# Left combinations of the split products formed in layer 0, products split from the second unit on, and w1 loaded a unit later

## The chip, the cores and the metric

The kernel runs on one core of one Trainium2 chip. The metric is the device time of one execution in microseconds (us). Times of a kernel are medians over several executions. One further execution was recorded by the hardware profiler; every row of a profile below is from that one execution.

## The reference

Two layers, each followed by a residual addition and a layer normalisation. All matrices are float32; N = 4096 nodes, D = 512 features. Cut to what matters:

```python
# layer 0
bw = sign(w0); ba = maximum(sign(x), 0)
x = layernorm(x + relu(adj @ (ba @ bw.T)))
# layer 1
node_att = softmax(x @ node_w, axis=0)
h = x @ edge_w
e = where(adj > 0, h @ h.T, -9e15)
support = x @ w1
out = (adj * node_att * softmax(e, axis=1)) @ support + bias
x = layernorm(x + out)
```

## The kernel before

The work is in four stages, one after the other on the tensor engine (PE).

**Layer 0** (0 to about 509 us). `xw = ba @ bw.T` is kept in SBUF. The 32 row blocks (128 rows each) of `adj @ xw` follow in the loop at L367. A row block has four quarters. In each, ScalarE (ACT) rounds a quarter of the adjacency tile `at` to `hi` (L385), VectorE (DVE) forms the rest `lo = at - hi` (L387), and PE multiplies both into the bank `acc` (L395, L396). `hi` and `lo` have two buffers each. What follows a row block (relu, residual, normalisation, node score, store of x1, transposes) is the generator `rest`. `step()` advances every unfinished `rest` once a quarter, after `lo` was formed, so the `rest` of block n runs in the four quarters of block n+1 and the first of n+2. Row blocks come in pairs; after the odd one of a pair, `left` (L338) forms the seven left operands of a Strassen-Winograd product (four additions of 128x256, L343 to L346) in the tile `sums_l`, and four DMAs of GpSimd's queue (L347 to L350) store them in `lop_d`. The order on DVE and ACT in this loop is the order in which the code is written (`manual_schedule`). DMAs that load `at` and `xb` are on SyncE's queue (SP), those that load pieces of the mask on ACT's queue, and all stores on GpSimd's queue (POOL).

**h** (509 to 606 us). `h = x1 @ edge_w` by the function `seven`, which calls `between_h` after each multiplication; DVE adds the seven products out of six PSUM banks.

**Scores** (606 to 1075 us). `h @ h.T`, masked row maxima and sums of exponentials, with the scores stored in `s_d`.

**Aggregation** (1075 us to the end). The product of the attention with x1, in 16 units `Aggregate(g, r)`: g is one of four groups of 1024 output rows, r one of four groups of 1024 terms of the sum, r innermost. A unit has seven products m (Strassen-Winograd on 2x2 blocks). The right operands are the weighted attention tiles `r11, r12, r21, r22` and the combinations t3, r12-r11, t2, t4 that `combine` forms on DVE (L896, L898, L901, L904; 128x2048 each). All of that for the next unit is done during a unit, by `steps()`: eight loads of 1 MB on POOL's queue (L858, L865), `shift` (DVE, L871), `exp` (ACT, L874), `clip` (ACT, L877), `weigh` (DVE, L883) and `combine`. For the first unit it is done at the end of the scores. The left operands are loaded from `lop_d` on SP's queue (L1097).

An unsplit product is 2 halves of 4 matmuls, 128x128 by 128x512 (L1117). A float32 matmul shows as two records in the trace, so this is 16 records. A **split** product is itself done by seven products of half the size: 14 matmuls by 128x256, 28 records. `SPLIT` names the three products m = 6, 4, 3 that are split, in the units for which `in_two(n)` holds, n = 4 to 14. A split product needs

- the right combinations of half size, `second` (DVE, L994 to L998, four of 128x512), in one of two tiles `extra` that are taken at unit 4;
- the left combinations of half size. `Aggregate.lefts` forms them once per r, in units 0 to 3 (g = 0), right after the product m whose left operand is in SBUF: four DVE instructions of 128x256 (L1007 to L1010), and two stores on ACT's queue (L1014) to `lop2_d`;
- from unit 4 on four loads per split product, L1101 to L1104, into two of the four `lop` buffers (`low`, `high`);
- four partial sums instead of two per product, each read back into a PSUM bank (`seed`, ACT, L1089) and written out again (`evict`, ACT, L1126); after the last unit of a g `join_inner` adds them up (21 additions of 128x256, L1165).

The program order in the aggregation is only a preference; the compiler's scheduler orders each engine's queue, except for instructions passed through `keep_in_program_order` (in unit 0: `pinned`). [...]

The matrix w1 is loaded into the tile `over` when the aggregation starts (L1391). `over` takes the place of `hT`, so the load waits for the last matmul of the scores. Four combinations of w1 (L1420 to L1423) are in the list `todo` of unit 1. They are used by `Finish` (L1244), the multiplication with w1 that follows each g.

## Time and profile before

| what | us |
|---|---|
| median of 3 runs | 1933.15 (1933.03 to 1934.24) |
| the profiled execution's own time | 1934.05 |
| span of its trace | 1932.3 |
| PE busy | 1913.5 |
| DVE busy | 1387.0 |
| ACT busy | 1024.3 |
| POOL busy | 280.5 |

The unit boundaries on PE, from the starts of the L1117 records (112 records in an unsplit unit, 148 in a unit with three split products):

| unit | PE from to, us | length |
|---|---|---|
| 0 | 1074.87 to 1126.85 | 51.98 |
| 1 | 1126.85 to 1174.92 | 48.07 |
| 2 | 1174.92 to 1222.98 | 48.06 |
| 3 | 1222.98 to 1271.92 | 48.94 |
| 4 | 1271.92 to 1323.57 | 51.65 |
| 5 | 1323.57 to 1383.50 | 59.93 |
| 7 | 1436.04 to 1482.51 | 46.47 |
| 11 | 1645.74 to 1692.21 | 46.47 |

Units 3, 7 and 11 hold 8 records of `panel` (L819) besides their own; units 4, 5 and others hold matmuls of `Finish`. In a timeline row the columns are start, length, engine, line and operation; in square brackets stands the idle time before it and what ended it. In a table of windows the columns are named in its first line; (x) is a count of instructions.

### The profile page before, as it was taken

Reading aid. Unit: us, or ns where it says so; the run is one execution under the profiler, and the core shown is the slowest. Engines: PE = TensorE matmul, PEld = TensorE weight load, DVE = VectorE, ACT = ScalarE, POOL = GpSimd, SP = SyncE. Lnnn points to the kernel's source line nnn. Section 1 sums busy time; section 2 is a strip of 40 time slices with the busy share of each in tenths; the row PEclk is TensorE's granted clock in tenths of the full one; section 3 lists DMA queues with packets and bytes.
Section 4 is the critical chain, followed back from the end, with each engine's and each line's share of the span. In section 5 each row is a group of like instructions: output and inputs, shape, how many; then the busy total and the mean of one; then the engine's idle time right before and its main releaser. Section 6 shows DMA issues by size and latency. Waiting matters only on the chain.

```text
span 1932.3 us, 20169 instructions
## 1 busy us (share of the span) xinstructions
PE 1913.5 (99%) x6708; PEld 1200.9 (62%) x6708; DVE 1387.0 (72%) x2058; ACT 1024.3 (53%) x1619; POOL 280.5 (15%) x409
## 2 busy tenths in 40 slices
PE   8999999999999999999999999999999999999998
PEld 6888888888644455444555444456666666666655
DVE  6766676666765567566664986687869987798746
ACT  5433333333202567576777665546767577757731
POOL 0122122222321101011111111111101101111100
PEclk9999999999999999999999999999999999999999
DMA  8888888888585478577773998787778787887731
GB/s 311 285 328 308 306 311 307 328 308 292 176 280 198 157 259 312 188 276 253 294 301 113 347 327 285 271 283 246 259 266 292 259 279 260 301 283 258 274 109 44
DMA packets 169527, 508.72 MB, mean 263 GB/s; under 512 B 15696, under 2 KB 41040, under 8 KB 161744
## 3 DMA queue, kind: packets, MB, share of 16 engines
q1 hardware_dynamic: 89472, 226.39, 34.6%
q0 software_dynamic: 64688, 239.10, 33.1%
q10 hardware_dynamic: 15264, 41.95, 6.0%
q8 instruction: 53, 0.87, 0.2%
q14 instruction: 50, 0.41, 0.1%
HBM read 385.74 MB, written 121.63 MB: 263 GB/s over the span
## 4 chain that ended last, share of the span: by engine, by line
PE 90%; DVE 4%; DMA 2%; issue 2%; ACT 1%; POOL 0%; ACTq 0%; DVEq 0%; POOLq 0%
PE bank L1117 33%; PE seven L749 14%; PE acc L395 11%; PE acc L396 11%; PE pe L676 6%; PE seven L101 5%; PE po L1244 3%; PE pt L638 3%; DMA slot<-s_d 1%; PE pt L355 1%; PE acc L236 1%; PE acc L235 1%; PE pw L213 1%; DMA over<-in_w_dram 1%; PE bank L1244 0%
## 5 line engine op out<-in xcount | busy, mean ns | idle before, releaser
L1117 PE MATMUL bank<-lent,lop 128*128 128x512 f32 (+1 forms) x1136 | 420.0, 517 | 0.0
L395 PE MATMUL acc<-xw,hi 128*128 128x512 f32 x960 | 376.5, 392 | 0.0
L396 PE MATMUL acc<-xw,lo 128*128 128x512 f32 x960 | 373.9, 390 | 0.0
L1117 PE MATMUL bank<-slot,lop 128*128 128x256 f32 (+1 forms) x1052 | 357.8, 488 | 1.9 <-DVE slot L898 1.9
L1117 PEld LDWEIGHTS bank<-lent,lop 128*128 128x128 f32 x1136 | 215.7, 190 | 173.9 <-issue 159.5
L1117 PEld LDWEIGHTS bank<-slot,lop 128*128 128x128 f32 x1052 | 200.2, 191 | 136.7 <-issue 116.6
L385 ACT CAST hi<-at 128x1024 fp32r<-128x1024 f32 x120 | 126.4, 1053 | 203.6 <-PE acc L395 152.9
L387 DVE TENSOR_TENSOR lo<-at,hi 128x1024 fp32r<-128x1024 f32 x120 | 148.0, 1233 | 85.7 <-ACT hi L385 85.7
L396 PEld LDWEIGHTS acc<-xw,lo 128*128 128x128 f32 x960 | 180.3, 188 | 36.8 <-DVE lo L387 0.3
L395 PEld LDWEIGHTS acc<-xw,hi 128*128 128x128 f32 x960 | 180.3, 188 | 36.8
L1126 ACT COPY over<-bank 128x512 f32<-128x512 f32 x200 | 115.0, 581 | 117.3 <-PE bank L1117 103.8
L676 PE MATMUL pe<-hT 128*128 128x512 f32 (+3 forms) x384 | 132.1, 486 | 0.0
L609 ACT ACTIVATE line<-line,nmax_c 128x512 f32<-128x512 f32 x160 | 114.8, 725 | 22.5 <-DVE nmax_c L600 22.3
L600 DVE CUSTOM_DVE_ANT_0 line<-lent,slot 128x512 f32<-128x512 bf16 x140 | 90.7, 688 | 47.7 <-ACT slot L686 26.7
L877 ACT ACTIVATE slot<-slot 128x2048 f32<-128x2048 f32 x36 | 68.8, 1911 | 73.6 <-DMA slot<-in_adj_t_dram 73.6
L871 DVE CUSTOM_DVE_ANT_1 lent<-lent,line 128x2048 f32<-128x2048 f32 x40 | 91.2, 2283 | 17.0 <-ACT line L831 8.6
L874 ACT ACTIVATE lent<-lent 128x2048 f32<-128x2048 f32 x40 | 76.5, 1913 | 49.1 <-DVE lent L871 49.0
L676 PEld LDWEIGHTS pe<-hT 128*128 128x128 f32 x384 | 64.6, 191 | 41.4 <-issue 33.8
L749 PE MATMUL seven<-hT 128*128 128x512 f32 x192 | 89.8, 593 | 0.0
L1089 ACT COPY bank<-over 128x512 f32<-128x512 f32 x144 | 84.7, 597 | 2.9 <-DVE left L1009 0.2
L638 PEld LDWEIGHTS pt<-ident,lent 128*128 128x128 f32 x418 | 52.3, 141 | 52.2 <-issue 38.3
L639 ACT COPY slot<-pt 128x512 f32<-128x512 f32 (+3 forms) x123 | 68.5, 560 | 22.9 <-PE pt L638 22.9
(261 smaller groups left out, 2828.2 us busy)
## 6 DMA issues: line engine op xcount, KB each, us to landing
at<-in_adj_t_dram SPq DMA_DIRECT2D x60, 1024.0 KB, 7.3
lop<-lop_d SPq DMA_DIRECT2D x79, 512.0 KB, 4.7
lent<-s_d POOLq DMA_DIRECT2D x39, 1024.0 KB, 7.3
slot<-in_adj_t_dram POOLq DMA_DIRECT2D x38, 1024.0 KB, 6.8
s_d<-slot POOLq DMA_DIRECT2D x30, 1024.0 KB, 7.2
lent<-in_adj_t_dram POOLq DMA_DIRECT2D x26, 1024.0 KB, 7.1
lop<-lop_d SPq DMA_DIRECT2D x99, 256.0 KB, 4.1
lent<-in_adj_dram SPq DMA_DIRECT2D x48, 512.0 KB, 5.0
```

The costliest lines, as they stand in the source:

```text
L101: nc.tensor.matmul(banks[bank][q], lop(m, q)[k], rop(m)[k], start=(first and k == 0), stop=(k == K - 1), skip_group_check=not first,)
L385: nc.scalar.copy(hi, aq)
L387: nc.vector.tensor_sub(lo, aq, hi.bitcast(F32))
L395: nc.tensor.matmul(acc, hi[:, c, :], xw[:, kb, :], start=(kb == 0), stop=False)
L396: nc.tensor.matmul(acc, lo[:, c, :], xw[:, kb, :], start=False, stop=(kb == NB - 1))
L609: nc.scalar.activation(line, line, AF.Exp, bias=nmax_c[:, b, c : c + 1], scale=-1.0, accum_out=sum_c[:, b, c : c + 1])
L638: nc.tensor.transpose(pt[:, j, :], src[:, ts(j, P)], ident)
L676: nc.tensor.matmul(pe[:, lo * P :], hT[:, k, ts(A * BG + i, P)], hT[:, k, (B * BG + lo) * P : (B + 1) * W], start=(k == 0), stop=(k == KD ...
L749: nc.tensor.matmul(ps, left[m][:, k, q, :], right[m][:, k, :], start=(first and k == 0), stop=(k == KD // 2 - 1), skip_group_check=not first,)
L871: pinned[0](nc.vector._custom_dve(TENSOR_ADD_SAT, out=q, in0=q, in1=m, s0=0.0, s1=-HUGE))
L1117: nc.tensor.matmul(ps, lop[:, k, :], rop[:, k, :], start=start, stop=(k == K - 1), skip_group_check=True)
L1126: nc.scalar.copy(self.to(), self.bank[:, : self.w])
```

## The change

Six edits.

1. `in_two(n)` holds for n = 1 to 14 (before: 4 to 14). The two `extra` tiles are taken at unit 1.
2. Unit 1 starts the partial sums (0, 5) and (6,) of its split products afresh; its other two are seeded with the sums that unit 0 has left, for which DVE subtracts the lower right from the upper right quarter, once per split product, after unit 0's last eviction of it.
3. `Aggregate.lefts` and its DMAs on ACT's queue are gone. In layer 0, for the row-block pairs that hold the second half of the terms (pair index modulo 4 of 2 or 3, so eight pairs), a generator `lefts` loads the left operands of the pair two before back from `lop_d` (two DMAs on POOL's queue), forms the combinations in place in two groups of four DVE instructions (128x128, then 128x256), and stores them in `lop2_d` (three DMAs on POOL's queue). It runs two row blocks after the odd block, one step a quarter; for the last pair the steps are called from `between_h`.
4. `lop2_d` is laid out so that a split product needs two loads of 512 KB, the whole left operand (`lop`) and the combinations (`inner`), in place of four.
5. w1 is loaded at unit 1, and its combinations are in `todo` at unit 2, in program order.
6. `SPLIT` names the same three products in another order, 4, 6, 3.

```diff
-SPLIT = 6, 4, 3
+SPLIT = 4, 6, 3
...
-    lop2_d = [dram.tile([P, len(SPLIT), 4, BG // 2, P], F32, name=f"lop2_d{g}") for g in range(HG)]
+    lop2_d = [dram.tile([P, len(SPLIT), BG // 2, 4, P], F32, name=f"lop2_d{g}") for g in range(HG)]
...
             scr = wp.tile([P, D], F32, name="scr", tag="scr")
+            inner = n % 2 and n // 2 % BG > 1 and lefts(n // 2, xb)
+            if inner:
+                next(inner)
             nc.vector.scalar_tensor_tensor(xb, acc, 0.0, xb, ALU.max, ALU.add)
...
             yield
             transpose_rows(b, xb)
+            if inner:
+                late.append(inner)
+                while n < NB - 1 and inner is not next(inner, inner):
+                    yield
+
+        late = deque()
+
+        def lefts(b, high):
+
+            to, of = lop2_d[b // BG][:, :, b % BG - 2], lop_d[b // BG][:, :, b % BG - 2, :]
+            low = wp.tile([P, len(SPLIT), HD], F32, name="low")
+            for k, m in ((slice(2), slice(4, 7, 2)), (2, 3)):
+                nc.gpsimd.dma_start(low[:, k, :], of[:, m, :])
+            for _ in range(3):
+                yield
+            for k, a, to_a in ((2, high[:, HD:], sums_l[:, 0, :]), (slice(2), sums_l[:, 1:4:2, :], None)):
+                to_a = a if to_a is None else to_a
+                (l11, l21), (l12, l22), (s4, s1) = ((x[..., :P], x[..., P:]) for x in (low[:, k, :], a, to_a))
+                nc.vector.tensor_add(s1, l22, l21)
+                nc.vector.tensor_sub(l21, l11, l21)
+                nc.vector.tensor_sub(l11, s1, l11)
+                nc.vector.tensor_sub(s4, l12, l11)
+                yield
+                nc.gpsimd.dma_start(to[:, k, :2], to_a.rearrange("p (n f) -> p n f" if k == 2 else "p k (n f) -> p k n f", f=P))
+            nc.gpsimd.dma_start(to[:, :, 2:], low.rearrange("p k (n f) -> p k n f", f=P))
...
         def between_h(q, n):
             count[0] += q is None
+            if q is None and count[0] > 1:
+                next(late[-1], None)
...
-        def lefts(self, m, lop):
...
-            tc.keep_in_program_order(nc.vector.tensor_add(s1, l21, l22))
-            tc.keep_in_program_order(nc.vector.tensor_sub(s2, s1, l11))
-            tc.keep_in_program_order(nc.vector.tensor_sub(s3, l11, l21))
-            tc.keep_in_program_order(nc.vector.tensor_sub(s4, l12, s2))
...
-            for n in range(2):
-                nc.scalar.dma_start(to[:, ts(n, 2)], s[n])
...
+            self.fresh = not unit.r or unit is blocks[1] and ns in ((0, 5), (6,))
...
-            if self.unit.r:
+            if not self.fresh:
...
-            if self.begin and not self.ns:
+            if self.begin:
                 lops["lop"] = lopp.tile([P, BG, HD], F32, name="lop")
                 nc.sync.dma_start(lops["lop"], lop_d[r][:, m])
-            elif self.begin:
-                low, high = (lopp.tile([P, 4, BG // 2, P], F32, name="lop2", tag="lop") for _ in range(2))
-                raw, s = lop_d[r][:, m], lop2_d[r][:, SPLIT.index(m)]
-                nc.sync.dma_start(low[:, :2].rearrange("p n b f -> p (n b) f"), raw[:, :, :P])
-                nc.sync.dma_start(low[:, 2:], s[:, :2])
-                nc.sync.dma_start(high[:, :2], s[:, 2:])
-                nc.sync.dma_start(high[:, 2], raw[:, BG // 2 :, P:])
+            if self.begin and self.ns:
+                lops["inner"] = lopp.tile([P, BG // 2, 4, P], F32, name="lop2", tag="lop")
+                nc.sync.dma_start(lops["inner"], lop2_d[r][:, SPLIT.index(m)])
...
-            start = not r and self.w == W
+            start = self.fresh and self.w == W
...
+                if u is blocks[0] and self.end and self.m in SPLIT:
+                    upper, lower = (sums[:, 0, self.m, h, W // 2 :] for h in range(2))
+                    nc.vector.tensor_sub(upper, upper, lower)
...
-        return HG <= n < len(blocks) - 1
+        return 0 < n < len(blocks) - 1
...
-    nc.sync.dma_start(w1_s, w1.rearrange("(k p) o -> p k o", p=P))
...
-        elif n == HG:
+        elif n == 1:
             extra.extend(take() for _ in range(2))
...
         if n == 1:
-            todo.append(lambda: nc.vector.tensor_sub(t3, r22, r12))
-            todo.append(lambda: nc.vector.tensor_sub(r12, r12, r11))
-            todo.append(lambda: nc.vector.tensor_sub(t2, r22, r12))
-            todo.append(lambda: nc.vector.tensor_sub(t4, r21, t2))
+            nc.sync.dma_start(w1_s, w1.rearrange("(k p) o -> p k o", p=P))
+        elif n == 2:
+            for o, a, b in ((t3, r22, r12), (r12, r12, r11), (t2, r22, r12), (t4, r21, t2)):
+                todo.append(lambda o=o, a=a, b=b: tc.keep_in_program_order(nc.vector.tensor_sub(o, a, b)))
```

More of the change, by code (lines that the diff above doesn't have):

```diff
@@ L999, in second @@
             yield
-        def lefts(self, m, lop):
-            (l11, l21), (l12, l22) = [[lop[:, k : k + 2, f : f + P] for f in (0, P)] for k in (0, BG // 2)]
-            s = [rows.tile([P, 2, BG // 2, P], F32, name="left2", tag="rows") for _ in range(2)]
-            s4, s3, s2, s1 = (x[:, n] for x in s for n in range(2))
-            tc.keep_in_program_order(nc.vector.tensor_add(s1, l21, l22))
-            tc.keep_in_program_order(nc.vector.tensor_sub(s2, s1, l11))
-            tc.keep_in_program_order(nc.vector.tensor_sub(s3, l11, l21))
-            tc.keep_in_program_order(nc.vector.tensor_sub(s4, l12, s2))
-            to = lop2_d[self.r][:, SPLIT.index(m)]
-            yield
-            for n in range(2):
-                nc.scalar.dma_start(to[:, ts(n, 2)], s[n])
         def right(self, m):
@@ L1023, in main @@
             halves = (None for m in [u.m for u in uses if u.ns and u.ns[0] == 1] for _ in self.second(m))
-            stores = deque()
             past = 0
@@ L1034, in main @@
                 past += u.work
-                if stores:
-                    next(stores.popleft(), None)
                 if not u.ns:
@@ L1040, in main @@
                     free.append(self.right(u.m))
-                    if not self.g and u.m in SPLIT:
-                        stores.append(self.lefts(u.m, lops["lop"]))
-                        next(stores[0])
                 between(past / whole, u.work)
-            if stores:
-                next(stores.popleft(), None)
         @property
@@ L1060 @@
     class Sums:
-        lefts = 0, 1, 2, 6, 5, 4, 3
         def __init__(self, unit, m, h=0, more=False, keep=False, ns=None):
@@ L1094, in multiply @@
             r, m = self.unit.r, self.m
-            if self.begin and not self.ns:
+            if self.begin:
                 lops["lop"] = lopp.tile([P, BG, HD], F32, name="lop")
                 nc.sync.dma_start(lops["lop"], lop_d[r][:, m])
-            elif self.begin:
-                low, high = (lopp.tile([P, 4, BG // 2, P], F32, name="lop2", tag="lop") for _ in range(2))
-                raw, s = lop_d[r][:, m], lop2_d[r][:, SPLIT.index(m)]
-                nc.sync.dma_start(low[:, :2].rearrange("p n b f -> p (n b) f"), raw[:, :, :P])
-                nc.sync.dma_start(low[:, 2:], s[:, :2])
-                nc.sync.dma_start(high[:, :2], s[:, 2:])
-                nc.sync.dma_start(high[:, 2], raw[:, BG // 2 :, P:])
-                lops["low"], lops["high"] = low, high
+            if self.begin and self.ns:
+                lops["inner"] = lopp.tile([P, BG // 2, 4, P], F32, name="lop2", tag="lop")
+                nc.sync.dma_start(lops["inner"], lop2_d[r][:, SPLIT.index(m)])
             if self.ns:
@@ L1108, in multiply @@
                 for k, n in enumerate(self.ns):
-                    at = self.lefts[n]
-                    lop = lops["high"][:, at - 4] if at > 3 else lops["low"][:, at]
+                    if n in (2, 4, 5, 6):
+                        lop = lops["inner"][:, :, n - 3 if n > 2 else 0, :]
+                    else:
+                        lop = lops["lop"][:, 2 * (n > 0) :, P * (n > 1) :][:, : BG // 2, :P]
                     products.append((self.bank[:, ts(k, W // 2)], lop, self.unit.halves[n], BG // 2))
```

## The prediction

> **What bounds the kernel now.** I read the page first: PE, busy 99%, and its row in the slices is at 9 except at both ends.
>
> ```profile
> PE 1913.5 (99%) x6708; PEld 1200.9 (62%) x6708; DVE 1387.0 (72%) x2058; ACT 1024.3 (53%) x1619; POOL 280.5 (15%) x409
> PE   8999999999999999999999999999999999999998
> ```
>
> So the time can only change by what PE does less, or by PE's idle time. For the first I took windows cut at the unit boundaries: unit 3 unsplit, unit 7 split, both with 8 `panel` records. Split is shorter, without idle time in either.
>
> ```profile
> core 0: us, PE busy (x) PEld busy (x) DVE busy (x) ACT busy (x) POOL busy (x), PEclk, DMA share, GB/s
> 1126.85:1174.92 48.07, 48.07 (x114) 21.28 (x113) 41.59 (x32) 31.87 (x34) 5.99 (x8) 1.00 0.88 312
> 1222.98:1271.92 48.94, 48.94 (x121) 22.10 (x120) 42.79 (x40) 28.28 (x35) 5.01 (x7) 1.00 0.74 255
> 1436.04:1482.51 46.47, 46.47 (x158) 28.94 (x157) 39.42 (x46) 34.15 (x48) 5.99 (x8) 1.00 0.86 307
> ```
>
> For the second I read PE's and DVE's timelines where the aggregation starts. PE stands still for 1.95 us for the product r12-r11 (L898). DVE had been idle 4.48 us before that: combinations of w1 (L1420, L1421), not needed before `Finish` some 200 us later, lie in its queue ahead of L896 and L898 and wait for w1.
>
> ```profile
> 1074.87 13.91 PE L1117 MATMUL bank<-slot,lop 128*128 128x512 f32 x32
> 1090.72 15.70 PE L1117 MATMUL bank<-slot,lop 128*128 128x512 f32 x32 [1.95 <-DVE slot L898]
> ...
> 1078.00 2.48 DVE L887 SCALAR_TENSOR_TENSOR slot<-lent,slot 128x512 f32<-128x512 f32 x4
> 1084.96 0.69 DVE L1420 TENSOR_TENSOR line<-over 128x512 f32<-128x512 f32 x1 [4.48 <-DMA over<-in_w_dram]
> 1085.57 2.28 DVE L896 TENSOR_TENSOR slot<-slot,slot 128x2048 f32<-128x2048 f32 x1
> 1087.78 0.69 DVE L1421 TENSOR_TENSOR over<-over 128x512 f32<-128x512 f32 x1
> 1088.38 2.29 DVE L898 TENSOR_TENSOR slot<-slot,slot 128x2048 f32<-128x2048 f32 x1
> ```
>
> The second PE row takes 15.70 us for the 32 records that took 13.91 before the gap. The windows say why: after the gap the clock is about halved.
>
> ```profile
> 1088.80:1090.70 1.90, 0.00 (x0) 0.00 (x0) 1.90 (x2) 1.30 (x1) 0.00 (x0) 1.00 1.02 397
> 1090.70:1094.20 3.50, 3.48 (x4) 1.46 (x5) 3.50 (x4) 1.57 (x3) 0.17 (x1) 0.52 1.02 392
> ```
>
> [...] 15.70-13.91 = 1.8 us lost. [...] L896 needs nothing of w1 and sits behind L1420. [...] SP: it stood 26.5 us at L1391, w1's load.
>
> **The change, part by part.** The sums are against the profiled execution: 1934.05 us, span 1932.3 and 1.75 around it. It lies 0.9 above the median 1933.15; I take that off at the end.
>
> *Three more split units.* Unit 3 less unit 7: 48.94-46.47 = 2.47 us (counting matmuls, three 512-wide ones of 0.858, would be 2.57). Units 1 to 3: 3 x 2.47 = **-7.4 us**, on PE and so on the path. Beside PE, per unit: DVE gains 12 half combinations of 0.683 (L994 to L998, 8.2 us) and loses 12 instructions of `lefts` (0.417, 5.0 us). Units 2 and 3 together have DVE busy 21.5+42.8 = 64.3 of 97.0 us (work moves from one to the other), so 73.5 of 92 after, w1's combinations included. Unit 1, at 41.6 of 48.1, is the full one, but it has inherited work: its own last combinations end at 1132.7, after its start, and unit 0's DVE is relieved of 12.3 us (4.5 wait, 2.8 w1, 5.0 `lefts`). Added in unit 0 and 1 are three subtractions like L1009 (0.416, 1.2 us) and three memsets of a bank, not in the trace; I take a 256-wide instruction for each, 0.42, with 0 and 0.69 (512-wide) as ends, all under PE. ACT gets an eviction of 0.58 and one of 0.38 in place of nothing, and up to the same in seeds: 1.9 x 3 = 5.8 us a unit, giving about 34 of 46 in units 2 and 3, as unit 7 shows (34.15).
>
> *w1 later.* L896 follows L887 at 1080.5 instead of 1085.6. L896 and L898 (2.2 us from start to start) then end at 1084.9; PE asks at 1088.8. The gap goes, 1.95, and the slow clock with it, 1.8: **-3.7 us**. Late next is L904 (t4), used last but one, over 20 us later. The load itself goes to SP in unit 1 (0.38 us issue, 10.7 to landing in the crowded unit 0), and the four combinations (2.8 us) to unit 2, some 50 us later, under DVE's free 26 us there. Uncovered, the 4.5 us wait would come back.
>
> *Left combinations in layer 0.* A pass has four DVE instructions of 128x128, about 0.29 each (estimate from L1009's 0.416 for 256 and L997's 0.683 for 512), and four of 0.42: 2.8 us; eight passes 22.5, against 48 x 0.417 = 20.0 removed from units 0 to 3. Counting the steps, the groups fall into the third and fourth quarter two row blocks after the odd block. There the block takes 14.98 us and DVE is busy 9.60:
>
> ```profile
> 403.15:418.13 14.98, 14.98 (x70) 12.41 (x69) 9.60 (x14) 4.89 (x6) 2.58 (x4) 1.00 0.94 337
> ...
> 411.74 1.22 DVE L387 TENSOR_TENSOR lo<-at,hi 128x1024 fp32r<-128x1024 f32 x1 [1.15 <-ACT hi L385]
> 415.36 1.23 DVE L387 TENSOR_TENSOR lo<-at,hi 128x1024 fp32r<-128x1024 f32 x1 [1.80 <-ACT hi L385]
> ```
>
> Idle are 1.15 and 1.80 us; the groups need 1.15 and 1.7. They fit. Beyond that PE has 1.3 us: a quarter is 3.6 us of PE, and `hi` and `lo` take 1.05+1.23 of it. Cost **0**. Five DMAs a pass go on POOL (busy 2.6 to 4.3 us of 15; 0.55 to 1.0 each). Two loads wait there for the stores of the pass before to land, about 7 us; behind them stand x1, `lop_d` and mask stores that become due over 7 us later. Traffic: 1.18 MB a pass, two passes within 60 us, so 39 GB/s more on 310 to 318; unit 0 reached 397.
>
> *Last pass, under h.* Its first group overwrites what L349 sends, issued at 517.1, landing 6.6 later, about 524. Behind it on DVE are the additions that free the PSUM bank PE wants at about 526 (508.7 + 5 x 3.44). Between 0 and 3 us; I take **+0.5** for this and the next part.
>
> *Loads of split products.* 1024 KB in two DMAs instead of 896 in four: SP issues 0.64 us instead of 1.6. But `inner` gets its buffer two partial sums later: in unit 8 the high half was issued at 1493.0 for a use at 1503.1, lead 10.1, now 8.4; the shortest lead was 7.9, now 6.2. A 512 KB load takes 4.7 us, at most 8.5 in the split units. So mostly covered; 0 to 2.3 us where not. ACT loses 24 store issues that it waited for.
>
> *g = 0's sums.* 21 more additions (0.42, 8.8 us of DVE) in unit 4. `Finish` shifts; it has a gap of 1.69 in unit 5. In units 8 and 9, where the 21 already exist, gaps are 0.29 and 1.44. **0**, with -1.7 to +2 as ends. The two `extra` buffers taken early: unit 2's t3 was ready 20 us before its unit, unit 7's, with them taken, 21. **0**.
>
> Sum: 1934.05 - 7.4 - 3.7 + 0.5 = 1923.45; less 0.9: **1922.6**.
>
> **Rivals.**
> (A) The gap stays: another input of unit 0 (attention tiles landed in 12 to 15 us there) takes w1's place. For: DMA share 1.02. Against: L887, the last step before L896, ended at 1080.5. 1922.6+3.7 = 1926.3.
> (B) New waits eat half: `inner` late in several of its 28 shortened loads, or h's stall with a slow clock behind it. For: leads down to 6.2. Against: no PE wait for `lop` today. 4 us: 1926.6.
> (C) Slower: DVE's first group in layer 0 waits. It overwrites what L349 sent; L349 was issued at 400.4, landing median 6.6, at most 8.9, so 407.0 to 409.3; the group's turn is 409.3. Later landing holds the next `lo`, and PE after 1.3 us. It turns the result at (11.1-0.5+3.9)/8+1.3 = 3.1 us beyond the margin, a landing of 12 us. POOL's loads in unit 0 took 12.2 at full DMA; then with half-clock spells of 1.8 each, 8 x (3.3-1.3+1.8) = 30: 1953. Against: layer 0 stays under 360 GB/s.
> (D) No change in sum: several of these together cost 8 to 14 us, about 1933. That split units are not shorter I exclude; units 7 and 11 both show 46.47.
>
> **How the numbers follow.** Forecast 0.62, A 0.14, B 0.14, C 0.05, D 0.05. Measurement tells 0.2%, 3.9 us, from no change: faster is below 1929.3, slower above 1937.0. Forecast, A and B are faster, less 0.02 for tails: 0.88; same 0.07; slower 0.05. The range's low end is the forecast less `Finish`'s 1.7, the 0.5, and the spread of the runs before (1.2), 1919; the high end is B with that spread, 1928. Beyond lie C, D and tails, 0.14.
>
> **What would show it.** Units 1 to 3 at 45.6, 45.6, 46.5 us without gaps; no L1420 ahead of L898, PE's first 64 aggregation records in 27.5 us; row blocks still 14.98 us; h still 97 us. Wrong if PE shows waits for `lo` around row blocks 7, 9, 15, 17, for `lop`, or at the start of h.

## The result and the profile after

| | before | after |
|---|---|---|
| median, us | 1933.09 (1931.40 to 1934.24, 4 runs) | 1946.70 (1942.15 to 1948.47, 4 runs) |
| ratio, 95% interval | | 1.0068 (1.0054 to 1.0082) |
| the profiled execution: own time, span | 1934.05, 1932.3 | 1942.15, 1940.3 |

The forecast was 1922.6, faster; the kernel became slower by 13.6 us in the median. The profiled execution of after is the fastest of its four; the other three have spans of 1943.4 to 1946.6 us at mean clocks of 0.996 to 0.994 (0.998 in the profiled one). So what the trace explains is the least that is lost.

PE's lines on the page of after: its busy time fell from 1913.5 to 1908.7 us, and the span grew. The loss is idle time.

```profile
PE 1908.7 (98%) x6816; PEld 1220.9 (63%) x6816; DVE 1422.8 (73%) x2137; ACT 1035.5 (53%) x1649; POOL 309.7 (16%) x449
PE   8999999999999999999999999999999999999998
```

The slices show nothing: the lost time is spread in pieces of 1 to 4 us. Windows cut at the unit boundaries find it (units 0, 1, 2, 3, and 4 to 6 in one).

```profile
core 0: us, PE busy (x) PEld busy (x) DVE busy (x) ACT busy (x) POOL busy (x), PEclk, DMA share, GB/s
1080.94:1129.02 48.08, 48.08 (x114) 21.29 (x114) 39.38 (x34) 26.29 (x33) 8.17 (x11) 1.00 0.90 332
1129.02:1181.85 52.83, 46.91 (x150) 27.71 (x149) 42.63 (x32) 32.74 (x43) 5.98 (x8) 1.00 0.75 270
1181.85:1227.70 45.85, 45.83 (x149) 28.04 (x148) 34.85 (x28) 31.59 (x42) 6.00 (x8) 1.00 0.84 296
1227.70:1274.17 46.47, 46.47 (x157) 28.94 (x156) 37.65 (x42) 32.82 (x47) 5.99 (x8) 1.00 0.80 294
1274.17:1441.85 167.68, 162.53 (x557) 105.14 (x556) 139.61 (x167) 107.27 (x136) 18.00 (x24) 1.00 0.76 264
```

| part | before | after | difference | forecast |
|---|---|---|---|---|
| up to the aggregation's start | 1074.87 | 1080.94 | +6.07 | +0.5 |
| unit 0 | 51.98 | 48.08 | -3.90 | -3.7 |
| unit 1 | 48.07 | 52.83 | +4.76 | -2.5 |
| unit 2 | 48.07 | 45.86 | -2.21 | -2.5 |
| unit 3 | 48.94 | 46.47 | -2.47 | -2.5 |
| units 4 to 6 | 164.12 | 167.68 | +3.56 | 0 |
| units 8 to 15 | 418.89 | 421.06 | +2.17 | 0 |

Three lines of the forecast hold (units 0, 2, 3) and four don't. In after the code of before has moved by some 30 lines: L1121 is the aggregation's matmul, L1096 `seed`, L1130 `evict`, L888 and L895 the loads of scores and mask, L901 `shift`, L904 `exp`, L907 `clip`, L913 `weigh`, L1024 to L1028 the right combinations of half size, L1251 and L1262 `Finish`'s matmul and its addition on DVE. In layer 0, L415 forms `lo`, L329 the node score, L334 stores x1, L352 is a load of the new `lefts`.

**Unit 0.** PE's timeline: the first 64 records took 27.64 us (forecast 27.5), without the gap of 1.95 us and without half clock (PEclk is 1.00 in the window above).

```profile
1080.94 27.64 PE L1121 MATMUL bank<-slot,lop 128*128 128x512 f32 x64
```

**Layer 0.** One gap and what follows it hold nearly all of the loss, at 81.4 us. First POOL's timeline in after, then one row of before, then DVE's timeline and windows across the gap (columns as above).

```profile
76.65 0.58 POOL L352 DMA_DIRECT2D low<-lop_d  x1 [7.11 <-DMA lop_d<-xb]
77.22 0.54 POOL L334 DMA_DIRECT2D x_d<-scr  x1
```

The same store in the kernel before:

```profile
72.52 0.57 POOL L331 DMA_DIRECT2D x_d<-scr  x1 [2.88 <-DVE scr L330]
```

DVE in after, and the windows:

```profile
83.60 0.69 DVE L329 CUSTOM_DVE_ANT_0 scr<-xb,nw_b 128x512 f32<-128x512 f32 x1 [4.84 <-DMA x_d<-scr]
84.21 0.08 DVE L329 DVE_READ_ACCUMULATOR2_ANT node_s<- 128x1 f32 x1
84.21 1.22 DVE L415 TENSOR_TENSOR lo<-at,hi 128x1024 fp32r<-128x1024 f32 x1
```

```profile
81.40:85.50 4.10, 0.01 (x2) 0.01 (x1) 1.90 (x4) 1.34 (x2) 0.00 (x0) 1.00 1.00 391
86.06:89.50 3.44, 3.44 (x10) 2.67 (x9) 2.51 (x3) 0.00 (x0) 2.63 (x4) 0.50 0.96 331
```

Read it from below: PE stood 4.1 us for `lo` and then ran 3.4 us at half clock (0.50 in the last window; 1.7 lost). `lo` stood on DVE behind L329, which overwrites `scr`; `scr` has one buffer, and the store of x1 still read it. That store was issued at 72.5 in the kernel before and at 77.2 here, behind L352 on POOL's queue. And L352, a load for the first pass of `lefts`, had waited 7.1 us for a store to `lop_d` to land. By the order of the program it belongs at about 115 us: on the queue it stands more than two row blocks ahead of that (a row block is 15 us). The order on this queue is the scheduler's, and the load waits for no engine, only for DMAs. It stands ahead of its place in four of the eight passes (first loads at 76.7, 195.4, 315.9 and 436.6 us), but only the first time did PE pay: at 195.4 the store behind it went out at 195.9, and DVE came to L329 at 203.3 only.

**Unit 1.** ACT's timeline, PE's after it, and POOL's:

```profile
1140.52 0.37 ACT L1130 COPY lent<-bank 128x256 f32<-128x256 f32 x1
1150.44 1.91 ACT L907 ACTIVATE slot<-slot 128x2048 f32<-128x2048 f32 x1 [9.55 <-DMA slot<-in_adj_t_dram]
1152.26 0.57 ACT L1130 COPY lent<-bank 128x512 f32<-128x512 f32 x1
```

```profile
1152.87 3.72 PE L1121 MATMUL bank<-lent,lop 128*128 128x256 f32 x16 [1.33 <-ACT lent L1130]
1158.47 3.70 PE L1121 MATMUL bank<-slot,lop 128*128 128x512 f32 x8 [1.88 <-ACT bank L1096]
```

```profile
1142.31 0.75 POOL L895 DMA_DIRECT2D slot<-in_adj_t_dram  x1 [12.09 <-DVE slot L913]
```

The mask tile for unit 2 was loaded at 1142.3, since its buffer came free only then, landed 8.1 us later, and ACT stood 9.55 us at its `clip` with evictions behind it. ACT is busy 32.74 of 52.83 us: it isn't short of time, it stands at the wrong instruction. The gap of 1.33 us ends with an eviction behind that `clip`. The one of 1.88 us has another wait behind it: its seed stands behind an `exp`, the `exp` behind a `shift` on DVE, and the `shift` had waited 5.77 us for scores. Five gaps of PE in this unit sum to 5.9 us.

**Units 4 to 6.** PE's waits there are all for `Finish`, its matmul for its addition on DVE. Before and after, with us in total, number and longest:

```profile
PE po L1244 <- DVE xb L1255: 2.2, 2, 1.7
PE po L1251 <- DVE xb L1262: 5.2, 5, 1.8
```

That is 3.0 of the 3.6 us. No half clock follows any of these waits in the profiled execution (PEclk is 1.00).

### The profile page after: what moved, and what is told of

Same layout as the page of the kernel before. It is cut to its first block, busy times and chain, and to the rows that moved or that the text cites. A ratio compares the mean times of both kernels' runs of the same rounds, so it can differ in the third digit from the quotient of the medians.

```text
span 1940.3 us, 20432 instructions
## 1 busy us (share of the span) xinstructions
PE 1908.7 (98%) x6816; PEld 1220.9 (63%) x6816; DVE 1422.8 (73%) x2137; ACT 1035.5 (53%) x1649; POOL 309.7 (16%) x449
## 4 chain that ended last, share of the span: by engine, by line
PE 75%; DVE 9%; issue 7%; DMA 6%; ACT 1%; POOL 1%; ACTq 0%; POOLq 0%; DVEq 0%
PE bank L1121 20%; PE seven L779 14%; PE acc L424 11%; PE acc L423 11%; PE pe L706 5%; PE seven L101 5%; PE po L1251 3%; DMA slot<-in_adj_t_dram 3%; PE pt L668 2%; DMA lent<-s_d 2%; DVE lent L913 1%; DVE lent L901 1%; PE acc L236 1%; PE acc L235 1%; PE pt L383 1%
## 5 line engine op out<-in xcount | busy, mean ns | idle before, releaser
L1121 PE MATMUL bank<-lent,lop 128*128 128x256 f32 (+1 forms) x1384 | 436.0, 465 | 3.5 <-ACT slot L907 1.8
L1121 PEld LDWEIGHTS bank<-lent,lop 128*128 128x128 f32 x1384 | 262.6, 190 | 151.5 <-issue 123.1
L1121 PE MATMUL bank<-slot,lop 128*128 128x512 f32 (+1 forms) x912 | 332.7, 510 | 2.4 <-ACT bank L1096 2.4
L1121 PEld LDWEIGHTS bank<-slot,lop 128*128 128x128 f32 x912 | 172.9, 190 | 134.4 <-issue 118.1
L415 DVE TENSOR_TENSOR lo<-at,hi 128x1024 fp32r<-128x1024 f32 x120 | 146.9, 1224 | 67.4 <-ACT hi L413 66.8
L1130 ACT COPY over<-bank 128x512 f32<-128x512 f32 x200 | 114.9, 582 | 82.9 <-PE bank L1121 80.2
L907 ACT ACTIVATE slot<-slot 128x2048 f32<-128x2048 f32 x42 | 80.4, 1913 | 102.2 <-DMA slot<-in_adj_t_dram 97.7
L901 DVE CUSTOM_DVE_ANT_1 lent<-lent,line 128x2048 f32<-128x2048 f32 x33 | 75.5, 2287 | 41.8 <-DMA lent<-s_d 33.6
L901 DVE CUSTOM_DVE_ANT_1 slot<-slot,line 128x2048 f32<-128x2048 f32 x31 | 70.7, 2285 | 21.6 <-DMA slot<-s_d 21.5
L1096 ACT COPY bank<-over 128x512 f32<-128x512 f32 x144 | 84.9, 598 | 2.5
L904 ACT ACTIVATE lent<-lent 128x2048 f32<-128x2048 f32 x33 | 63.1, 1913 | 38.1 <-DVE lent L901 37.9
```

Source lines behind the costliest of these rows:

```text
L415: nc.vector.tensor_sub(lo, aq, hi.bitcast(F32))
L901: pinned[0](nc.vector._custom_dve(TENSOR_ADD_SAT, out=q, in0=q, in1=m, s0=0.0, s1=-HUGE))
L1121: nc.tensor.matmul(ps, lop[:, k, :], rop[:, k, :], start=start, stop=(k == K - 1), skip_group_check=True)
L1130: nc.scalar.copy(self.to(), self.bank[:, : self.w])
```

## The experiments

All ratios are against runs of the kernel before on the same chip; before's medians there were 1931.9 to 1932.8.

### First four: the parts, one at a time

Theory 1: unit 1 stalls because the two `extra` buffers are taken early, so that unit 2's loads come late. Theory 2: a split unit 1 has too much for ACT and DVE in any case. For layer 0: the hoisted loads are the cause.

**w1 later alone** (e1_w1_later): before with edit 5, and nothing else.

> The kernel before with the later load of w1 alone (edit 5). If the wait for w1 was the cause of unit 0's gap, unit 0 takes 48.1 us instead of 52.0 and the whole 1.9 + 1.8 = 3.7 us less, 1929.4. If another input of unit 0 takes its place (rival A of the prediction), no more than 1 us is gained.

1930.25 us (12 runs), ratio 0.9995 (0.9986 to 1.0003); span 1928.1. Unit 0 is 48.08 us, no gap; units 1 to 3 and 4 to 6 as before. In the trace the whole 3.9 us is gained. In the medians it's 2.5 us, and by the interval not told from none. Two other kernels, the next one and the one with `Finish` later, explain a part of that: they leave w1 where it was, and in their traces unit 0 lost 1.4 and 1.7 us, by gaps of 1.18 and 1.43 us with no half clock after them. The execution that I predicted from had a worse gap than these, by chance as far as the traces tell.

**Buffers early alone** (e4_buffers_early): before, with

```diff
-        elif n == HG:
+        elif n == 1:
             extra.extend(take() for _ in range(2))
```

> The kernel before, but the two tiles extra are taken at unit 1 instead of unit 4; nothing is split earlier and nothing else changes. Theory 1: units 1 or 2 grow by 2 to 6 us, with ACT waiting at clip for a load that GpSimd's queue issued late. Theory 2: units 1 to 3 stay at 48.1, 48.1 and 48.9 us, and the time at 1933.

1931.70 us (12 runs), ratio 0.9997 (0.9989 to 1.0006). Unit 1 in the windows, and ACT's longest waits in it:

```profile
1124.32:1172.38 48.06, 48.06 (x113) 21.28 (x112) 33.58 (x27) 25.80 (x28) 5.99 (x8) 1.00 0.82 297
```

```profile
ACT slot L877 <- DMA slot<-in_adj_t_dram: 11.4, 3, 5.1
ACT lent L874 <- DVE lent L871: 4.2, 1, 4.2
```

The loads for unit 2 are as late as in after (issued at 1136.6 to 1138.5, 12 to 14 us into the unit; in before, two of them at 1117 and 1127), and ACT waits 11.4 us for masks in all (13.6 in after), though 5.1 at most at once (9.55 in after). PE doesn't notice. So loads as late as these alone don't stall an unsplit unit.

**Idle memory for unit 1** (e2_idle_memory): after, but units 1 to 3 use a part of `over` that is idle then, and the two buffers are taken at unit 4.

```diff
-        elif n == 1:
+        elif n == HG:
             extra.extend(take() for _ in range(2))
...
+    def spare_of(g):
+        return extra if g else [sums[:, 1, m : m + 2].rearrange("p m h w -> p (m h) w") for m in (3, 0)]
```

> The changed kernel, but for g = 0 the two tiles extra lie in a part of the tile over that is idle until unit 4, so that units 1 to 3 keep all 13 buffers for attention tiles; the real extra tiles are taken at unit 4. Theory 1 (the two buffers missing in unit 1 hold back the loads for unit 2, and ACT stands at clip with evictions and seeds behind it): unit 1 takes 45.6 to 46.5 us instead of 52.8, the whole 6 to 7 us less than the changed kernel. Theory 2 (ACT and DVE have too much to do in unit 1 because of the split products themselves): unit 1 stays above 51 us.

1950.88 us (4 runs), ratio 1.0095 (1.0080 to 1.0110). Unit 1 takes 58.96 us, more than in after; two of its three largest gaps (3.60 and 2.41 us) now end with DVE's L1027 and L1024, which stand on DVE behind a `shift` that waited 6.2 us for scores, and behind the combinations that waited with it; the third (2.40) ends with a seed on ACT. Theory 1, that the two buffers are the cause of the stall, has fallen, and with it the cure that I had in mind. Theory 2 isn't shown either: DVE is busy 49.4 of 59.0 us there.

**Loads pinned** (e3_loads_pinned): after, with

```diff
-                nc.gpsimd.dma_start(low[:, k, :], of[:, m, :])
+                tc.keep_in_program_order(nc.gpsimd.dma_start(low[:, k, :], of[:, m, :]))
```

> The changed kernel, but the two loads of low keep their program order on GpSimd's queue, so the first of them stands behind the x1 stores of the row blocks before instead of ahead of one. Theory (layer 0 loses its time because x1's store stands behind a load that waits for lop_d to land, and scr, which that store reads, is wanted again on DVE): no PE wait for lo in layer 0, layer 0 and h end 5.8 to 6.1 us earlier than in the profile of the changed kernel, and the runs spread less. Rival (the traffic, or the wait of the first group for sums_l): layer 0 keeps waits of several us.

1938.10 us (7 runs), ratio 1.0027 (1.0016 to 1.0039): 8.6 us under the median of after, which is of another series. The runs don't spread less, against what I expected (6.0 us over seven runs, 6.3 over four in after). The aggregation starts at 1075.01 us, as in before. POOL's and DVE's timelines at the same place:

```profile
72.58 0.57 POOL L334 DMA_DIRECT2D x_d<-scr  x1 [3.01 <-DVE scr L333]
77.72 0.76 POOL L378 DMA_DIRECT2D lop_d<-sums_l  x1 [4.56 <-DVE sums_l L373]
```

```profile
78.74 0.69 DVE L329 CUSTOM_DVE_ANT_0 scr<-xb,nw_b 128x512 f32<-128x512 f32 x1
79.36 0.08 DVE L329 DVE_READ_ACCUMULATOR2_ANT node_s<- 128x1 f32 x1
79.36 1.22 DVE L415 TENSOR_TENSOR lo<-at,hi 128x1024 fp32r<-128x1024 f32 x1
```

x1 is stored on time, L329 waits for nothing, and the first L352 is issued at 115.0. Layer 0's loss is the hoisted load: the eight passes of combinations themselves cost nothing. Unit 1 is 54.29 us here (one half-clock spell more than in after: PEclk is 0.58 from 1167.10 to 1171.00, and 24 records take 10.44 us where they take 8.83 in after), units 4 to 6 are 169.59.

### Unit 1

Theory 3, after these: three things meet. Unit 1 takes over a backlog from unit 0 (its own last combination starts at 1131.7 in the kernel with pinned loads, 8.6 us into the unit). The loads for unit 2 are late. And the wait for them on ACT, 9.35 us long, meets the short partial sums of split products. By the lengths of its records such a product gives PE 6.0 us of work in four banks, so I estimate that six banks hold at most 9 us (the expectation below has about 8, an estimate too); an unsplit one gives 6.9 us in two, so six hold 20.6 by the same estimate. All the kernels below have pinned loads.

**Split from unit 2** (e8_from_unit2_pinned): `return 1 < n < ...` in `in_two`, and the three places that name unit 0 or 1 moved by one.

> The kernel after with layer 0's two loads kept in program order, and split products from unit 2 on instead of unit 1. Theory 3 (unit 1 stalls because three things meet there: it takes over unit 0's backlog, so that its own combinations end some 8 us after its start; the loads for unit 2 come late, because the two buffers are gone; and ACT's wait for such a load, 9.35 us long, stands ahead of evictions, for which a split unit's six banks give PE only about 8 us of work, where an unsplit unit's give twice that): a unit later there is no backlog, as in unit 4 of the kernel before. Unit 1 at 48.1 us, units 2 and 3 at 45.6 to 46.5 without gaps over 0.6, about 8 us less than the 148.5 of these three in the kernel with pinned loads: 1930. Rival 3a (whichever unit is first to be split, with the buffers gone, stalls): unit 1 at 48.1, unit 2 at 51 to 54, and 1936 to 1939.

1934.80 us (15 runs), ratio 1.0017 (1.0009 to 1.0024). Units 1, 2 and 3 in the windows:

```profile
1123.28:1171.34 48.06, 48.06 (x113) 21.28 (x112) 38.57 (x27) 27.67 (x33) 5.23 (x7) 1.00 0.62 213
1171.34:1217.59 46.25, 45.84 (x150) 28.04 (x148) 30.37 (x24) 27.89 (x37) 5.24 (x7) 1.00 0.87 310
1217.59:1264.67 47.08, 46.74 (x157) 28.86 (x156) 37.77 (x42) 32.73 (x47) 5.98 (x8) 1.00 0.81 294
```

The stall didn't move to unit 2: 141.4 us for the three units against 148.5. Theory 3 holds against 3a. The trace bears out its third part: ACT has a wait of 9.13 us for a mask here as well, from 1165.9 to 1175.0, but it falls on the last product of the unsplit unit 1 and the first of unit 2, which isn't split, and PE has no gap there. Whether the backlog is needed too isn't told apart. The median, 1934.8, is above the expected 1930; the excess is in units 4 to 6.

**Unit 1's steps later** (e10_steps_later): in unit 1 all steps for unit 2 but its loads of scores come 0.13 of a unit later.

```diff
+            if n == 1:
+                first = deque(sorted(((min(1.0, f + 0.13) if f not in (0.14, 0.28) else f, s) for f, s in first), key=lambda x: x[0]))
```

> The kernel with pinned loads; in unit 1 the steps that prepare unit 2 (its loads of scores apart) come 0.13 of a unit later in the program, so that fewer of ACT's and DVE's waits for late loads stand ahead of evictions and seeds. Theory 3: ACT's longest wait for a load in unit 1 falls from 9.35 us to below 6, the first three gaps (1.2, 1.8 and 0.5 us) shrink, and unit 1 falls from 54.3 us to 47 to 51; 1931 to 1935. Theory 2 (a split unit 1 has too much to do for ACT and DVE, whatever they wait for): unit 1 stays above 52.5 us and the time at 1937 to 1939, or more where unit 2 then starts late.

1942.47 us (4 runs), ratio 1.0055 (1.0038 to 1.0071). Unit 1 fell to 50.18 us, within what Theory 3 said and not what Theory 2 said. But its other signs failed: ACT's longest wait for a mask is still 7.4 us, and of the first three gaps only one shrank (1.2 to 0.7 us). What went is a later gap of 1.76 us with the half clock behind it (the 24 records of 10.44 us take 8.83). Unit 2 grew from 46.4 to 48.9 us, and units 4 to 6 from 169.6 to 172.5. The time is a miss.

**Clips on DVE** (e11_clips_on_dve): in unit 1, `weigh` takes the maximum with 0 itself (four DVE instructions of 512 in place of one of 2048) and ACT doesn't clip.

> The kernel with pinned loads; the mask tiles of unit 2 are clipped within DVE's product (four instructions of 512 in place of one of 2048) and not by ACT, so that in unit 1 ACT never waits for a mask's load. Theory 3: the gaps that end with an eviction behind ACT's clip (1.2 and 1.8 us) go, those behind its exp, which waits for DVE and a late load of scores (1.8 and 0.5), may stay: unit 1 at 49 to 52 us, 1933 to 1936. Rival 3b (the wait just moves: DVE now stands for the masks with the half combinations behind it): unit 1 at 53 us or more, its gaps ended by DVE's L1024 to L1028, 1938 or more.

1942.69 us (4 runs), ratio 1.0062 (1.0047 to 1.0077). Unit 1 is 48.45 us. The gaps that had ended with an eviction behind `clip` (1.2 and 1.8) are gone, those behind `exp` (2.0 and 0.4) are there, as Theory 3 had it for each; unit 2, where ACT clips again, now has the gap behind ACT's seeds (2.55 us, then half clock: eight records in 3.63 us where eight of the same size take 1.89) and takes 51.3. So the wait on ACT is the cause of those gaps, and taking it away at one place hands the lateness on to the next. The time is a miss, as large as rival 3b had it, though unit 1 isn't.

### Units 4 to 6

Their code is nearly that of before, but of the kernels so far every one with a split unit 3 took 167.5 to 172.5 us for them, all others 162.6 to 164.1. What is new in them is that the 21 additions for g = 0 put off the first `Finish`: its first matmul comes 32.7 us into unit 4 in after, 24.1 in before.

**No additions for g = 0** (e9_no_joins_g0): the kernel with pinned loads, but it leaves out the 21 additions that join the sums of the split products of g = 0, so its output isn't the whole result.

> The kernel with pinned loads, without the 21 additions that join the split products of the first column half (left out of the computation, so the output is not the whole result). Theory F (these additions on DVE put off the first Finish by some 10 us, to where its steps meet a DVE that stands for late loads): units 4 to 6 together fall from 169.6 us to at most 166, Finish starts before 1300 us from the span's start, and the time falls by 3 to 5 us to 1933 to 1935. Rival Fa (the waits of Finish come from something else, such as the lack of buffers or the order of the queues): units 4 to 6 stay within 1 us of 169.6 and the time at 1937 to 1939.

1937.60 us (6 runs), ratio 1.0029 (1.0018 to 1.0041). Units 5 and 6 went from 117.1 to 111.0 us (before: 112.5), with one gap of 1.0 us; but unit 4 has a gap of 2.63 us with half clock behind it (eight records in 5.29 us where eight ahead of the gap take 3.60) and takes 56.4 (before: 51.6). In all 167.5: neither theory as stated.

**All but the splits** (e12_all_but_splits): the change with pinned loads, units 1 to 3 unsplit.

> The kernel after with layer 0's two loads kept in program order and units 1 to 3 unsplit again: what is left of the change is the left combinations in layer 0, their two loads a product, the new choice of the split products, and w1 later. Theory: with the loads pinned these parts cost and give nothing beside w1's 3.7 us: units 1 to 3 at 48.1, 48.1 and 48.9, units 4 to 6 together at 162.6 to 164.2, span 1928 to 1929, 1930 to 1931.5. Rival (the new loads or the new choice of products is behind the loss in units 4 to 6): these at 167 to 170, and 1933 to 1936.

1931.22 us (20 runs), ratio 0.9995 (0.9989 to 1.0002). Units 1 to 3 at 48.07, 48.07, 48.94; 4 to 6 at 162.61. The left combinations in layer 0, the new loads and the new order of products cost nothing up to unit 7. (Units 8 to 15 take 421.9 us in this trace, 418.9 in before; more on that below.)

**Split from unit 3** (e14_from_unit3): as from unit 2, one later.

> The kernel with pinned loads, split products from unit 3 on. It has the 21 additions of the first column half, but only one more split unit. If these additions, which put Finish off by some 10 us, are enough for the loss: units 4 to 6 at 167 to 170, unit 3 at 46.5, and 1933 to 1935. If the loss needs the two buffers to be missing since unit 1 or 2: units 4 to 6 at 163 to 165, and 1928 to 1930.

1938.71 us (8 runs), ratio 1.0031 (1.0020 to 1.0041). Unit 3 at 46.47, units 4 to 6 at 171.9: one more split unit gains 2.5 us and costs 9. That the buffers are taken as early as unit 1 or 2 isn't needed for the loss.

**Shifts later where Finish runs** (e13_shifts_later): from unit 2; the four `shift` 0.06 of a unit later in these units, so that DVE would wait less ahead of `Finish`.

> The kernel split from unit 2 with pinned loads; in every unit that Finish falls in, the shifts of the next unit's scores come 0.06 of a unit (about 3 us) later in the program, so that DVE waits less for their loads with Finish's products behind it. Theory G (units 4 to 6 lose 5 us since Finish's results on DVE stand behind a shift that waits for a late load; a gap of 1.4 to 2.3 us and as much again at half clock): the three gaps over 1 us shrink to under 1, units 4 to 6 fall from 169.4 to 163 to 166, and 1929 to 1932. Rival Ga (the shifts just take other places, and other steps of Finish stand behind them): 168 to 172, and 1934 to 1937.

1934.82 us (12 runs), ratio 1.0013 (1.0002 to 1.0023). Units 4 to 6 at 173.2, with gaps of 1.4, 2.3 and 3.1. Rival Ga, and a little worse than it said: other steps stand in the way instead.

**Finish later in the kernel before** (e15_finish_later): four empty entries ahead of the first `Finish`.

> The kernel before, with four empty entries in the list of things to do ahead of the first Finish: no work is added or taken, only the first Finish comes four steps (some 10 us) later. Theory G (it's where Finish falls between the waits for the next unit's loads that decides): units 4 to 6 grow from 164.1 us to 166 to 170, and 1935 to 1938. Rival Gb (the place of Finish doesn't matter, the loss comes with the split units' use of memory): 163 to 165 as before, and 1932 to 1934.

1932.14 us (12 runs), ratio 0.9995 (0.9986 to 1.0004). Units 4 to 6 at 162.9, no loss, as rival Gb had it; Theory G as stated missed. So "later" isn't bad by itself. What is left of G is for kernels with a split unit 3, and the next ones ask there.

**Finish moved, no work added** (e16_finish_2_later, e16_finish_4_later, e16_finish_6_later): the kernel split from unit 2, with

```diff
+            todo.extend([lambda: None] * (4 if n == 3 else 0))
             todo.append(lambda f=second: (f.load((0, 2)), f.load((1, 3))))
```

and 2 or 6 in place of 4.

> The kernel split from unit 2 with pinned loads, and two empty entries ahead of the first Finish, which comes some 5 us later; no work is added. Theory G2 (in the kernels with a split unit 3 the place of Finish against DVE's waits for loads decides): the three kernels of this series differ from 169.4 us for units 4 to 6 by more than 3 us among themselves, at least one of them at 162 to 165; for this one 163 to 170. Rival H (the way in which split units use memory makes the loads late, wherever Finish is): all three at 167 to 172, 1933 to 1937.

> The same with four empty entries, some 10 us later. Theory G2: 162 to 170 for units 4 to 6, by place; rival H: 167 to 172.

> The same with six empty entries, some 15 us later. Theory G2: 162 to 170 for units 4 to 6, by place; rival H: 167 to 172.

**Additions four at a time** (e17_joins_4_a_step): `for _ in range(2 if n > HG else 4)`, so `Finish` comes earlier.

> The kernel split from unit 2 with pinned loads; up to unit 4 the additions that join the split products go four at a time on DVE instead of two, so that the first Finish comes a step or two earlier. Theory G2: units 5 and 6 go towards the 111 us of the kernel without these additions (116.96 here), while unit 4 may get a gap as that one did: 165 to 169 in all, 1931 to 1934. Rival H: 168 to 171, 1933 to 1936.

| kernel, split from unit 2 | units 4 to 6, us | median, us | ratio, 95% interval |
|---|---|---|---|
| Finish as it is | 169.4 | 1934.80 (15 runs) | 1.0017 (1.0009 to 1.0024) |
| additions four at a time | 163.4 | 1932.34 (12) | 0.9999 (0.9990 to 1.0007) |
| Finish 2 steps later | 168.5 | 1933.29 (20) | 1.0006 (0.9999 to 1.0013) |
| Finish 4 steps later | 164.5 | 1930.38 (12) | 0.9987 (0.9978 to 0.9996) |
| Finish 6 steps later | 167.6 | 1938.89 (5) | 1.0038 (1.0025 to 1.0051) |

(With six steps, eight of `Finish`'s records fall into unit 7, 1.7 us more there, and in its trace units 8 to 15 take 8.4 us more than with four, so units 4 to 6 are the smaller part of what that kernel loses.) Additions four at a time put the first `Finish` back to 24.1 us into unit 4. Theory G2 holds against H: with the same matmuls, additions and loads, units 4 to 6 move between 163.4 and 169.4 us with the place of `Finish`. Each of these is one execution, but the low figure comes back in the two kernels below (163.7 and 164.8), and the kernels with the two lowest figures have the two lowest ratios. The start of the first `Finish` isn't all of it: the kernel without additions for g = 0 has it at 24.1 us too and took 167.5. What a bad place looks like, in the kernel split from unit 2: DVE's timeline, then PE's, then POOL's.

```profile
1374.46 2.29 DVE L901 CUSTOM_DVE_ANT_1 lent<-lent,line 128x2048 f32<-128x2048 f32 x1 [2.60 <-DMA lent<-s_d]
1376.67 0.48 DVE L1262 SCALAR_TENSOR_TENSOR xb<-po,f,xb 128x256 f32<-128x256 f32 x1
```

```profile
1373.86 1.03 PE L1251 MATMUL po<-line,line 128*128 128x256 f32 x4
1377.20 1.24 PE L1251 MATMUL po<-over 128*128 128x256 f32 x4 [2.32 <-DVE xb L1262]
1378.23 5.23 PE L1121 MATMUL bank<-lent,lop 128*128 128x512 f32 x8
```

```profile
1365.73 0.75 POOL L888 DMA_DIRECT2D lent<-s_d  x1 [12.09 <-PE bank L1121]
```

A product of `Finish` adds onto the bank `po` of the one before, so PE waits until DVE's L1262 has read it. L1262 stands behind a `shift` (2.29 us) that waits for scores, whose load waited for a buffer that PE was still using. The gap is 2.32 us, and the next eight records take 5.23 us at half clock where eight ahead of the gap take 3.60 at full: 4 us for one collision. Such waits of DVE are there in every kernel, and by themselves they cost nothing (10.6 us of waits for scores in units 4 to 6 of before, 9.1 in this kernel); it matters whether one of `Finish`'s additions is behind one. But they are shorter too where `Finish` stands well: 4.9 us with additions four at a time, 5.5 with four steps. The runs don't part these two effects of its place.

Four steps later is the only kernel of the study whose interval lies below 1: 0.13% faster than before, and 16 us faster than after, in medians of different series. It is one of eighteen intervals and wasn't repeated.

### Do they add up?

**Unit 1 split, the other two cured** (e19_from_unit1_joins_4): after with pinned loads and additions four at a time.

> The kernel after with two cures, pinned loads in layer 0 and the additions four at a time up to unit 4, unit 1 still split. If the three causes add up: aggregation starts at 1075.1, unit 1 takes 52.5 to 54.3 us, units 4 to 6 take 163 to 165, and the time is some 5 us below the kernel with pinned loads alone, 1932 to 1935. If they don't (a cure in one place moves the loss to another): 1936 or more.

1935.01 us (18 runs), ratio 1.0016 (1.0008 to 1.0023). The aggregation starts at 1075.16, unit 1 takes 51.6 us (its stall stays, a little shorter), units 4 to 6 take 164.8. They add up, roughly, at the upper end of what was expected: the second cure takes 4.8 us off units 4 to 6 in the traces and 3.1 off the median, where about 5 were expected.

**From unit 3, additions four at a time** (e18_from_unit3_joins_4).

> Split products from unit 3 on, pinned loads, the additions four at a time up to unit 4. If the place of Finish was the whole of the loss in the kernel split from unit 3 (171.9 us for units 4 to 6): units 1 to 3 at 48.1, 48.1 and 46.5, units 4 to 6 at 162 to 165, and 1928 to 1930.5, a gain of 2 to 4 us on the kernel before. If not: units 4 to 6 above 166.5 and 1932 to 1936.

1930.91 us (13 runs), ratio 0.9995 (0.9987 to 1.0004); units 1 to 3 at 48.07, 48.07, 46.47, units 4 to 6 at 163.7 in place of 171.9. The units are as expected and the place of `Finish` was the whole of the loss there; the time is just above what was expected, and not told from before.

What the earlier splits are worth, once the losses around them are cured, hardly shows in the medians. Units 1 to 3 are 2.8 us shorter than in before when split from unit 2, and 2.5 us when split from unit 3 (traces of the two kernels with additions four at a time). But their ratios are 0.9999 and 0.9995, and all but the splits had 0.9995.

## Why the prediction was wrong

In the profiled execution the forecast's sum, 1923.45, misses 18.7 us. By its own steps:

- **Three more split units, -7.4.** Right for units 2 and 3 (45.86 and 46.47 us; forecast 45.6 and 46.5), wrong for unit 1: 52.83, 7.2 us more than forecast. The step that failed is "Unit 1, at 41.6 of 48.1, is the full one, but it has inherited work". I weighed DVE's busy time there, and the sum was about right (42.6 us after); but I didn't ask how long ACT and DVE stand at waits (ACT 9.55 us at one `clip`), nor what is queued behind these. Nor did I see that a split product more than halves the time that PE's banks cover (9 us for 20.6, by the estimate above). "The two `extra` buffers taken early ... 0" is right by itself (the kernel with only that kept its time). That it is wrong beside the split isn't shown: with the buffers given back unit 1 was longer still (58.96).
- **w1 later, -3.7.** The mechanism is right: 3.9 us in unit 0. The size is that of one execution. Two others with w1 unmoved had lost 1.4 and 1.7 us there, and the edit alone gave 0.9995 (0.9986 to 1.0003).
- **Left combinations in layer 0, 0.** Measured: 6.1 us, 4.1 of a gap and 1.7 of half clock. The step that failed: "behind them stand x1, `lop_d` and mask stores that become due over 7 us later". I took the place of the two loads on POOL's queue from the order of the program. The first was hoisted ahead of an x1 store that was due at once, and the store went out behind it at 77.2 us, after the load's wait of 7.1 us (72.5 in the kernel before). Pinned, the part costs 0 as forecast. Rival C put a wait into layer 0 too, but another one (for `sums_l`) in each pass; the one that came happened once, at 81.4 us, ahead of all the row blocks that I had named for it.
- **Last pass under h and the loads of split products, +0.5.** PE was idle 0.1 us in 97 of h, as before, and never waited for `lop`. The loads that rival B feared for came in time.
- **g = 0's sums, 0 with -1.7 to +2 as ends.** Measured: +3.6 us, and 5.3 to 5.5 with pinned loads and the split from unit 1 or 2. I saw that `Finish` would shift, and took the bounds from other gaps of `Finish`. The step that failed is that bound: I didn't count that several collisions can come at once (five waits in after), nor that half clock nearly doubled the cost of a gap of 2 us once in each of the two kernels with pinned loads (1.7 us behind 2.18, 1.6 behind 2.32).
- **Units 8 to 15** weren't in the sum; they cost 2.2 us more. Between 418.6 and 429.6 us stand in the traces, with gaps at `Finish` as in units 4 to 6. The four kernels with the old loads and the old order of products took at most 419.2, all the others at least 420.3, the one with units 1 to 3 unsplit too (421.9). So the new loads or the new order may be behind it, which no kernel tests alone.

The sum: 5.6 (layer 0 beyond the 0.5) - 0.2 (unit 0) + 7.2 + 0.3 (units 2 and 3) + 3.6 + 2.2 = 18.7. Of the rivals, D had the kind (several costs together) but too small a size, and C the direction; I gave each 0.05. None of them named a hoisted load or a shortened cover.

Left open: why the other runs of after are 3 to 6 us longer than the profiled one. Their clocks are lower by 0.002 to 0.004; a spell of 3.4 us at half clock lowers the mean by 0.001, so two to four more such spells would fit, an estimate that no trace of theirs shows. The profiled execution has four gaps of 1.76 to 1.88 us with full clock behind them, where other runs may have had spells. Open too is why units 8 to 15 differ.

## What to carry to other kernels

When an instruction that waits is added, look for it in the queue as it runs, not in the program: here a load that waits for no engine was put far ahead, and the store behind it on its queue went out at 77.2 us in place of 72.5. When work is cut into smaller pieces, price the cover too: the same six banks hold less than half the time by my estimate (9 us for 20.6), and an ACT wait that cost nothing across unsplit products (9.13 us) ended in a stall of PE in a split unit (9.55). Where two chains share an engine (here `Finish` and the next unit's loads on DVE), an edit that moves one against the other can be worth several us either way (units 4 to 6 took 163.4 to 169.4 us with the place of `Finish`); try a few places of it with no work added before judging the edit itself.

## What the runs showed of the hardware

**Half clock after a gap of PE.** A gap needn't be long for half clock to follow it. Over all traces of this case: of 41 gaps of 1.3 to 1.75 us none was followed by a spell at half clock, of 18 between 1.76 and 2.05 us four were, of 13 between 2.05 and 2.5 us eight, and of 8 longer ones all. The shortest of these with a spell behind it is one of 1.76 us (in unit 1 of the kernel with pinned loads, 0.58 from 1167.10 to 1171.00); behind a gap of the same length in unit 1 of after the clock is 1.00 (1173.20 to 1178.00). Behind 2.40 us in the kernel with idle memory it is 1.00 too (1144.50 to 1149.50). So between 1.76 and 2.5 us the length of a gap alone doesn't tell whether a spell follows; what else decides isn't shown.

A spell lasted 3.4 us in the profiled executions of before and after (0.52 from 1090.70 to 1094.20, 0.50 from 86.06 to 89.50). In the kernel with idle memory the half clock around a gap of 1.19 us held longer (0.54 from 1174.30 to 1179.00, 0.50 from 1177.20 to 1181.00: by my estimate from these two windows, 6.3 of the 6.7 us). Single spells cost 1.6 to 1.8 us (5.23 us for 3.60 above, 15.70 for 13.91 in the prediction).

**Order on an engine and on a queue.** In the stalls shown above what stood behind a waiting instruction started after it: the eviction that PE waited for at 1152.26, at the end of the `clip` that had waited 9.55 us for its mask; `lo` at 84.21, at the end of L329, which had waited 4.84 us for the store of x1; and on POOL's queue that store at 77.22, behind a load that had waited 7.11 us. With that load pinned the store went out at 72.58, and L329 waited for nothing.
